# Linear attention with a mixture of experts: the last rounds re-ordered, with one shared expert and eight outputs held back, bulk loads, late stores, and experts shared out by work left

## The chip, the cores and the metric

The kernel runs on one core of one Trainium2 chip. Its time is the device time of one execution in microseconds, and the median of several runs is compared. A profile of one further execution gives the span from the first to the last instruction, and what each engine did in it. TensorE multiplies matrices (PE in the profile; PEld is its loading of weights), VectorE is DVE, ScalarE is ACT, GpSimd is POOL, SyncE is SP. Each engine works through its own instructions in the order written; engines wait for one another by semaphores. All data are 32-bit floats.

## The reference

The input has 4 sequences of 1024 tokens with 256 channels, so 4096 tokens. Each token is normalized, and the result is the sum of the input, an attention block and a feed-forward block, both of the normalized tokens:

```python
xn = _layernorm(x, axis=-1)
x = x + attention(xn, ...) + feed_forward(xn, ...)

# attention: 16 heads of 16 channels
sq, sk = elu(q) + 1, elu(k) + 1
local = causal_linear_attention(q, k, v)        # chunks of 128, running state S and z per head
a_c / n_c                                       # coarse: sum of 4 memory banks, read by sq
out_fine = (outs * softmax(rel)).sum(0)         # the 4 banks one by one, weighed per batch
gprob = sigmoid(relu(coarse @ eg_w1.T + eg_b1) @ eg_w2.T + eg_b2)
memory = gprob * out_fine + (1 - gprob) * coarse
output = (gate * memory + (1 - gate) * local) @ w_o.T

# feed forward: 8 routed experts of 176 hidden channels, the best 2 for each token, and a shared one of 352
cw = two largest of softmax(xn @ gate_weight.T), scaled to sum 1
y = sum over e of cw[e] * (silu(xn @ w_gate[e].T) * (xn @ w_up[e].T)) @ w_down[e].T
y = y + (silu(xn @ sw_gate.T) * (xn @ sw_up.T)) @ sw_down.T
```

## The kernel before

The 4096 tokens are 32 tiles of 128 (`NTT`), and 4 tiles make a block of 512 (`NT`, 8 blocks, `NBLK`). First all blocks are loaded, normalized and transposed; the normalized rows also go to a table `xns` in DRAM. The routing sorts the 8192 pairs of token and expert by expert into 71 groups of 128 slots (`NST`); a group has one expert. A second table in DRAM, `sums`, starts as a copy of the input. Every value tile of a block (`wide`) comes from the pool `big`, tag `tok`, with 8 buffers, one a block.

Then come 34 rounds, one for each tile and two to finish. `attention_round(n)` lists the units of round n: `scores` (TensorE), four `mask`s (DVE), `turned` (transposes for the output of tile n-2 and the gate of tile n-1), `keys_back`, `output(n-2)`, `memory` and `weigh`, `gate_hidden`, `fine`, `local`, `gate_out`, `back` and `update`. Attention has six additions and products on POOL a round: `cg` (in `weigh`), `fm` and two for `diff` (in `fine`), `loc` (in `back`), `state` (in `update`). The score tile `quad` in PSUM is one for all rounds. `output` adds the shared expert's product and the attention's `w_o` product into one PSUM tile. Beside a round stand the key, query and shared-expert projections of the next blocks (`beside`), four rounds for each block, and in rounds 4 to 29 the routed experts (`side`).

A group j of an expert has four steps: `expert_turn` (transposes; it also issues the gather of rows four groups ahead on POOL, `fetch_rows`, L990, and the loads of weights three groups ahead on SP, `fetch_weights`, L1001 to L1009), `expert_hidden` (TensorE, L1036, then ACT and DVE), `expert_out` (TensorE, L1049, then ACT scales it into `y`, three buffers), and `put`. `put` (L1058) is an indirect DMA on POOL that adds the 128 rows of `y` onto `sums`. Two such scatters may hit the same row, so each waits until the one before has landed.

`experts()` lists the units of all groups with weights, `split` cuts the list into 26 parts of equal weight, and `mix` merges lists so that each advances evenly by weight; the merged order is the order in which all engines get their instructions. There is no other scheduler.

The last 8 tiles (from `held_from`, 24) have no `output` in their rounds: their transposed attention `oT` is kept, and the outputs come in the tail, after the last `put`. Tiles before that have their output without the experts in `acc`, held in SBUF. The tail has two kinds of units. `residual(n)` loads a tile's rows of `sums`, and `output(n, True)` adds them and stores the tile from ACT's queue. `experts_part(n)` loads two tiles of `sums` into an expert's weight buffer on SP, and `total(n)` adds them to `acc` on POOL (L980) and at once issues the store on ACT's queue (L981). These totals are mixed evenly over rounds 30 to 33. Every load of `sums` waits for the last `put`.

Of the kernel before, what the change touches and what calls it, by code (L numbers as in the profile page):

```python
# [8 lines left out]
FP = mybir.dt.float32  # L9
# [5 lines left out]
P = 128  # L15
NT = 4
# [6 lines left out]
def linear_attention_moe_kernel(  # L23
# [28 lines left out]
    nc = tc.nc  # L52
    T, H = x.shape
# [3 lines left out]
    NC = H // P  # L57
# [12 lines left out]
    NBLK = T // TB  # L70
    NTT = T // P
# [3 lines left out]
    VW = NH * D1 + CW - D1  # L75
# [19 lines left out]
    st = {}  # L95
# [56 lines left out]
    sums = dram.tile([T + P, H], FP, tag="sums", name="sums")  # L152
# [8 lines left out]
    for e in range(E):  # L161
# [4 lines left out]
        out=before_t, in_=ones, compare_op=ALU.is_gt, fill=0.0,  # L166
# [5 lines left out]
        out=causal, in_=ones, compare_op=ALU.is_ge, fill=0.0,  # L172
# [5 lines left out]
        out=own, in_=ones[:, :HC], compare_op=ALU.is_ge, fill=0.0,  # L178
# [3 lines left out]
        out=own, in_=own, compare_op=ALU.is_ge, fill=0.0,  # L182
# [487 lines left out]
    def at(n):  # L670
        blk, i = divmod(n, NT)
        return blk, i, slice(i * P, (i + 1) * P)
# [180 lines left out]
    def turned(n):  # L853

        srcs = [(s, m) for s, m in (("o", n), ("coarse", n + 1)) if 0 <= m < NTT]
        pt = bank(f"pt2_{n}").rearrange("p (s c t) -> p s c t", s=2, t=P)
        for s, key in enumerate(srcs):
            src = st.pop(key)
            for c in range(NC):
                nc.tensor.transpose(pt[:, s, c, :], src[:, c * P : (c + 1) * P], ident)  # L860
        dst = tmp.tile([P, 2, NC, P], FP, tag="oc", name=f"oc_{n}")
        copied = slice(0, len(srcs))
        if n >= held_from:
            oT = tmp.tile([P, NC, P], FP, tag="oT", name=f"oT_{n}", bufs=NTT - held_from)
            nc.scalar.copy(oT, pt[:, 0])
            copied = slice(1, len(srcs))
        if copied.start < copied.stop:
            nc.scalar.copy(dst[:, copied], pt[:, copied])  # L868
        for s, (what, m) in enumerate(srcs):
            st["oT" if what == "o" else "cT", m] = dst[:, s]  # L870
        if n >= held_from:
            st["oT", n] = oT
# [62 lines left out]
    held_from = NTT - 2 * NT  # L935

    def residual(n):

        res = tmp.tile([P, H], FP, tag="res", name=f"res_{n}", bufs=3)
        nc.sync.dma_start(res, sums[n * P : (n + 1) * P, :])  # L940
        st["res", n] = res

    def output(n, last):

        blk, i, tok = at(n)
        if i == 0:
            st["acc", blk] = io.tile([P, NT, H], FP, tag="xnT", name=f"acc_{blk}")
        acc = st["acc", blk][:, i, :]
        oT = st.pop(("oT", n))
        po = bank(f"po_{n}")  # L950
        for f in range(NF):
            k = min(P, FS - f * P)
            nc.tensor.matmul(  # L953
                po[:, :H], st["h", blk, f][:k, tok], wd[:k, f, :], start=(f == 0), stop=False
            )
        for c in range(NC):
            nc.tensor.matmul(  # L957
                po[:, :H], oT[:, c, :], wo[:, c, :], start=False, stop=(c == NC - 1)
            )
        if last:  # L960
            nc.vector.tensor_add(acc, po[:, :H], st.pop(("res", n)))  # L961
            nc.scalar.dma_start(out[n * P : (n + 1) * P, :], acc)  # L962
        else:
            nc.scalar.copy(acc, po[:, :H])

    def experts_part(n):

        tag, parts = ("wgu", [P, NC, 2, F]) if n % 4 else ("wdn", [P, 2, H])
        flat = "p a b c -> p (a b c)" if n % 4 else "p a b -> p (a b)"
        res = exw.tile(parts, FP, tag=tag, name=f"part_{n}").rearrange(flat)  # L970
        res = res[:, : 2 * H].rearrange("p (n h) -> p n h", h=H)
        nc.sync.dma_start(
            res, sums[n * P : (n + 2) * P, :].rearrange("(n p) h -> p n h", p=P)
        )
        st["part", n] = res

    def total(n):
        blk, i, _ = at(n)
        acc = st["acc", blk][:, i : i + 2, :]
        nc.gpsimd.tensor_add(acc, acc, st.pop(("part", n)))  # L980
        nc.scalar.dma_start(  # L981
            out[n * P : (n + 2) * P, :].rearrange("(n p) h -> p n h", p=P), acc
        )


# [81 lines left out]
    first_round, last_round = 4, 30  # L1067

    def mix(*streams):

        rank = []
        for k, stream in enumerate(streams):
            whole = sum(u[0] for u in stream)
            done = 0
            for u in stream:
                rank.append(((done + u[0] / 2) / whole, k, len(rank), u))
                done += u[0]
        return [u for _, _, _, u in sorted(rank, key=lambda r: r[:3])]

    def run(units):  # L1080
        for _, f, *args in units:
            f(*args)
# [20 lines left out]
    def shared(blk):  # L1103
        units = []
        for f in range(NF):
            units += [
                ((1024, shared_gate, blk, f), None),
                ((1024, shared_up, blk, f), (64, shared_hidden, blk, f)),
            ]
        return units  # L1110
# [10 lines left out]

    def projections(blk):

        pairs = keys(blk) + (queries(blk + 1) if blk + 1 < NBLK else []) + shared(blk)
        units = [u for pair in pairs for u in pair]
        if blk % BPB == 0:
            b = blk // BPB
            at = units.index(pairs[3][1]) + 1
            units[at:at] = [(64, mean_queries, b)]
            at = units.index(pairs[6][0])  # L1130
            units[at:at] = [(64, batch_weights, b)]
        return [u for u in units if u]
# [21 lines left out]
    def experts():  # L1154
        units = [(2000, lambda: None), (256, expert_turn, -2), (256, expert_turn, -1)]
        for j in range(NST + 1):
            if j < NST:
                units += [(704, expert_hidden, j)]
            units += [(64, put, j - 2)] if j > 1 else []
            units += [(512, expert_out, j - 1)] if j > 0 else []  # L1160
            units += [(512, expert_turn, j)] if j < NST else []
        return units + [(64, put, NST - 1)]

    def totals():
        ahead = 5
        pairs = list(range(0, held_from, 2))
        units = [(10, experts_part, n) for n in pairs[:ahead]]
        for k, n in enumerate(pairs):
            if k + ahead < len(pairs):
                units += [(10, experts_part, pairs[k + ahead])]  # L1170
            units += [(64, total, n)]
        return units

    def split(units, parts):

        whole = sum(u[0] for u in units)
        runs = [[] for _ in range(parts)]
        done = 0
        for u in units:
            runs[min(parts - 1, int((done + u[0] / 2) * parts / whole))].append(u)  # L1180
            done += u[0]
        return runs


    ahead = "S0 S1 masks N0 T0 S2 S3 N1 N2 V0 T1 T2 S4 memories V1 S5 N3 N4 V2 T3 T4 S6 gates V3 S7"
# [5 lines left out]
    with tc.tile_pool(name="ps_v", bufs=2, space=bass.MemoryType.PSUM) as ps_v:  # L1191
        for what in ahead.split():
# [3 lines left out]
            blk = int(what[1:])  # L1196
# [31 lines left out]
    rounds = [attention_round(n) for n in range(NTT + 2)]  # L1228
    beside = [[u for pair in shared(1) for u in pair if u]] + [projections(blk) for blk in range(2, NBLK)]
    beside = [units for run_of in beside for units in split(run_of, NT)] + [[]] * (NT + 2)  # L1230
# [12 lines left out]

    side = split(experts(), last_round - first_round)
    for n in range(first_round, last_round):
        run(mix(*[u for u in (rounds[n], beside[n], side[n - first_round]) if u]))

    units = [(10, residual, n) for n in range(held_from, held_from + 3)]  # L1250
    outs = {n: [(1280, output, n, True)] for n in range(held_from, NTT)}
    for n in range(held_from, NTT - 3):
        outs[n] += [(10, residual, n + 3)]
    ready = last_round - 2
    units += [u for n in range(held_from, ready) for u in outs[n]]

    units[2:2] = [(1800, lambda: None)]
    tail = mix([u for n in range(last_round, NTT) for u in rounds[n]], units)

    tail += mix(rounds[NTT], [u for n in range(ready, NTT - 1) for u in outs[n]])  # L1260
    tail += rounds[NTT + 1] + outs[NTT - 1]
    run(mix(tail, totals()))


# [54 lines left out]
```

## Time and profile before

| | |
|---|---|
| median of 3 runs | 736.98 us (736.46 to 739.15) |
| the profiled execution itself | 731.18 us |
| its span, first to last instruction | 729.5 us |
| mean granted clock of TensorE | 0.967 |
| busy: PE, PEld | 653.1, 465.3 us (90%, 64%) |
| busy: DVE, ACT, POOL | 455.9, 266.8, 386.0 us (62%, 37%, 53%) |
| DMA | 81.51 MB, 112 GB/s on the mean |
| scatter `put` L1058 | 71 of 1597 ns on POOL, 113.4 us |
| gather L990 | 71 of 994 ns on POOL, 70.6 us |

How to read it. The page cuts the span into 40 slices of 18.2 us and gives each engine's busy share in tenths; PE has 9 nearly throughout, and 2 in the third slice from the end. A row of groups or of the timeline has the start (timeline only), the busy time, the engine, the line of the kernel, the operation, what it writes and from what, and in brackets the idle time of the engine just before and what ended it. A row of waits has the waiting engine and line, the releaser, the total time, the number of times and the longest. PE's records overlap, since matmuls are pipelined; the spacing of their ends is the truer price. The span of a POOL instruction is rough.

### The profile page before, as it was taken

The page shows a single profiled execution, that of the slowest core. Times are in us where ns is not written, and L with a number is a line of the kernel's source. Part 1 is how long each engine was busy: PE and PEld are TensorE (multiplying, and loading weights), DVE is VectorE, ACT ScalarE, POOL GpSimd, SP SyncE. Part 2 cuts the span into 40 slices and gives each one's busy share as a digit, 9 for nine tenths or more (in the row PEclk, how much of TensorE's full clock was granted, in tenths as well). Part 3 has the DMA queues.
Part 4 walks back from the last instruction along what each step waited for, and adds up shares of the span by engine and source line. Part 5 has one row for each costly group of instructions (what it writes and reads, how often), then busy time and mean ns, then how long its engine had stood idle before and what let it go on. Part 6 is the DMA issues. An engine that isn't in the chain of part 4 may idle for free. (4 is left out here: it accounts for less than half of the span.)

```text
span 729.5 us, 14268 instructions
## 1 busy us (share of the span) xinstructions
PE 653.1 (90%) x5084; PEld 465.3 (64%) x5084; DVE 455.9 (62%) x1193; ACT 266.8 (37%) x614; POOL 386.0 (53%) x436
## 2 busy tenths in 40 slices
PE   3599986879999999999999999999999998997295
PEld 3485465756676776766676767666776665676274
DVE  6444888984656665665666646656666556667262
ACT  3365443423433443334433443344332433333010
POOL 3210034553656675655566666466664656666464
PEclk9799989999999999999999999999999999999598
DMA  9456000013444564454444544454554545552563
GB/s 292 156 198 190 0 1 1 2 52 89 106 116 99 123 127 96 104 119 106 116 116 107 128 109 120 93 129 101 122 126 96 134 112 108 130 127 40 153 200 123
DMA packets 86563, 81.51 MB, mean 112 GB/s; under 512 B 7629, under 2 KB 84093, under 8 KB 86365
## 3 DMA queue, kind: packets, MB, share of 16 engines
q1 hardware_dynamic: 67629, 57.00, 27.3%
q0 software_dynamic: 13632, 18.62, 15.5%
q10 hardware_dynamic: 5232, 4.99, 2.0%
q8 instruction: 40, 0.66, 0.4%
q14 instruction: 30, 0.25, 0.1%
HBM read 62.62 MB, written 22.15 MB: 116 GB/s over the span
## 5 line engine op out<-in xcount | busy, mean ns | idle before, releaser
L1058 POOL DMA_INDIRECT sums<-y,islot x71 | 113.4, 1597 | 70.6 <-DMA sums<-y,islot 15.1
L1042 DVE SCALAR_TENSOR_TENSOR hidden<-hidden,phe 128x176 f32<-128x176 f32 x71 | 23.8, 335 | 122.4 <-ACT hidden L1041 122.4
L1036 PE MATMUL phe<-wgu,turned 128*128 128x352 f32 x276 | 96.9, 474 | 2.5 <-ACT turned L1029 2.1
L698 DVE TENSOR_TENSOR sT<-quad,causal 128x512 f32<-128x512 f32 x128 | 80.4, 681 | 8.3 <-PE quad L691 7.8
L828 POOL TENSOR_TENSOR cg<-coarse,gates 128x256 f32<-128x256 f32 x32 | 24.3, 760 | 109.3 <-DVE h L883 61.1
L990 POOL DMA_INDIRECT xg<-xns,islot x71 | 70.6, 994 | 17.7 <-issue 9.7
L1049 PE MATMUL pye<-wdn,turned 88*128 88x256 f32 x284 | 75.5, 388 | 4.2 <-PE pu L786 3.0
L1036 PEld LDWEIGHTS phe<-wgu,turned 128*128 128x128 f32 x276 | 48.5, 191 | 26.2 <-issue 6.4
L1049 PEld LDWEIGHTS pye<-wdn,turned 88*128 88x128 f32 x284 | 50.1, 189 | 20.1 <-issue 8.5
L1053 ACT ACTIVATE y<-pye,wslot 128x256 f32<-128x256 f32 x71 | 33.6, 473 | 70.6 <-PE pye L1049 70.3
L846 POOL TENSOR_TENSOR fm<-fm 128x512 f32<-128x512 f32 x32 | 41.7, 1304 | 26.2 <-DVE prob L892 13.1
L1041 ACT ACTIVATE hidden<-phe 128x176 f32<-128x176 f32 x71 | 22.6, 318 | 86.7 <-PE phe L1036 79.7
L1029 ACT COPY turned<-pte 128x512 f32<-128x512 f32 (+1 forms) x71 | 41.2, 580 | 35.6 <-PE pte L1027 34.6
L953 PE MATMUL po<-wd,h 128*128 128x256 f32 (+1 forms) x192 | 49.5, 395 | 0.8 <-ACT oc L868 0.7
L905 PE MATMUL pg<-xnT,wg 128*128 128x512 f32 (+1 forms) x96 | 48.2, 627 | 0.0
L919 PE MATMUL psu<-xnT,wu 128*128 128x512 f32 (+1 forms) x96 | 46.1, 603 | 0.5 <-DVE loc L751 0.5
L835 DVE TENSOR_TENSOR fm<-quad,rw 128x512 f32<-128x512 f32 x64 | 42.2, 680 | 0.0
L953 PEld LDWEIGHTS po<-wd,h 128*128 128x128 f32 (+1 forms) x192 | 35.8, 196 | 7.7 <-ACT oc L868 1.2
L362 PE MATMUL pv<-wvg,xnT 128*128 128x264 f32 x128 | 33.1, 420 | 8.2 <-ACT xnT L347 8.2
L560 POOL TENSOR_TENSOR held<-ones,two 128x213 f32<-128x213 f32 (+1 forms) x22 | 16.0, 737 | 44.5 <-DVE ones L540 44.5
L806 PE MATMUL quad<-mem,sqT 32*128 32x170 f32 x512 | 27.6, 328 | 9.1 <-DVE sT L698 9.1
L894 DVE SCALAR_TENSOR_TENSOR o<-diff,prob,loc 128x256 f32<-128x256 f32 x32 | 33.1, 1035 | 3.4
(210 smaller groups left out, 1374.5 us busy)
## 6 DMA issues: line engine op xcount, KB each, us to landing
wgu<-in_w_gate_dram SPq DMA_DIRECT2D x71, 176.0 KB
wgu<-in_w_up_dram SPq DMA_DIRECT2D x71, 176.0 KB
wdn<-in_w_down_dram SPq DMA_DIRECT2D x71, 176.0 KB
x<-in_x_dram SPq DMA_DIRECT2D x8, 512.0 KB
xns<-x SPq DMA_DIRECT2D x8, 512.0 KB
sums<-in_x_dram SPq DMA_DIRECT2D x8, 512.0 KB
part<-sums SPq DMA_DIRECT2D x12, 256.0 KB
out_dram<-acc ACTq DMA_DIRECT2D x12, 256.0 KB
```

The lines of the kernel that those rows point to most:

```text
L698: nc.vector.tensor_mul(sT, quad[:, g, :].rearrange("p (c t) -> p c t", t=P), causal[:, None, :].to_broadcast([P, NC * 2, P]),)
L835: nc.vector.tensor_mul(fm[:, c].rearrange("p g m (r k) -> p g (m r) k", k=HD), quad[:, :, c * KM + KX + KN : (c + 1) * KM].rearrange("p g ...
L846: nc.gpsimd.tensor_add(fm[:, :, 0:2, :], fm[:, :, 0:2, :], fm[:, :, 2:4, :])
L905: nc.tensor.matmul(pg[:n, :], wg[:, k, f * P : f * P + n], xnT[:, k, :], start=(k == 0), stop=(k == NC - 1),)
L919: nc.tensor.matmul(pu[:n, :], wu[:, k, f * P : f * P + n], xnT[:, k, :], start=(k == 0), stop=(k == NC - 1),)
L953: nc.tensor.matmul(po[:, :H], st["h", blk, f][:k, tok], wd[:k, f, :], start=(f == 0), stop=False)
L990: nc.gpsimd.indirect_dma_start(out=xg, out_offset=None, in_=xns, in_offset=bass.IndirectOffsetOnAxis(ap=islot[:, j : j + 1], axis=0),)
L1029: nc.scalar.copy(dst[:, lo:hi], pt[:, lo:hi])
L1036: nc.tensor.matmul(ph[:, : 2 * F], xgT[:, k, :], wgu[:, k].rearrange("p g f -> p (g f)"), start=(k == 0), stop=(k == NC - 1),)
L1049: nc.tensor.matmul(py[:, :H], hT[:FH, f, :], wdn[:, f, :], start=(f == 0), stop=(f == 1))
L1053: nc.scalar.activation(y, py[:, :H], AF.Copy, scale=wslot[:, j : j + 1])
L1058: nc.gpsimd.indirect_dma_start(out=sums, out_offset=bass.IndirectOffsetOnAxis(ap=islot[:, j : j + 1], axis=0), in_=st.pop(("y", j)), in_of ...
```

## The change

- The shared expert of the last block (`shared(7)`) is no longer among the projections beside rounds 24 to 27; it is mixed with round 30.
- The experts are cut by work left: each round from 4 to 29 gets as many weight units of experts as it lacks to a common level, at most 1.5 times the mean.
- All loads of `sums` are issued together after round 29: two residual loads of four tiles each, then twelve loads of two tiles.
- Residuals, the kept `oT` and six of the twelve parts are placed in buffers of the early value tiles (`big`, tag `tok`); the other six parts stay in expert weight buffers (`in_weights`).
- No total stands in round 30. They are mixed evenly over what follows round 30, and their stores are on SP's queue, each behind the next total. The eight outputs follow in rounds 31, 32 and 33 (three, three, one, and the last by itself), and each of their stores is on ACT's queue, one output later.

```diff
@@ -861,7 +861,9 @@
         dst = tmp.tile([P, 2, NC, P], FP, tag="oc", name=f"oc_{n}")
         copied = slice(0, len(srcs))
         if n >= held_from:
-            oT = tmp.tile([P, NC, P], FP, tag="oT", name=f"oT_{n}", bufs=NTT - held_from)
+            if n % NT == 0:
+                st["oTs"] = big.tile([P, NT, VW], FP, tag="tok", name=f"oT_{n}")
+            oT = st["oTs"][:, n % NT, : NC * P].rearrange("p (c t) -> p c t", t=P)
             nc.scalar.copy(oT, pt[:, 0])
             copied = slice(1, len(srcs))
         if copied.start < copied.stop:
@@ -936,9 +938,12 @@
 
     def residual(n):
 
-        res = tmp.tile([P, H], FP, tag="res", name=f"res_{n}", bufs=3)
-        nc.sync.dma_start(res, sums[n * P : (n + 1) * P, :])
-        st["res", n] = res
+        res = big.tile([P, NT, VW], FP, tag="tok", name=f"res_{n}")[:, :, :H]
+        nc.sync.dma_start(
+            res, sums[n * P : (n + NT) * P, :].rearrange("(n p) h -> p n h", p=P)
+        )
+        for i in range(NT):
+            st["res", n + i] = res[:, i]
 
     def output(n, last):
 
@@ -959,27 +964,38 @@
             )
         if last:
             nc.vector.tensor_add(acc, po[:, :H], st.pop(("res", n)))
-            nc.scalar.dma_start(out[n * P : (n + 1) * P, :], acc)
         else:
             nc.scalar.copy(acc, po[:, :H])
 
     def experts_part(n):
 
+        if n < 3 * NT:
+            if n % NT == 0:
+                st["parts"] = big.tile([P, NT, VW], FP, tag="tok", name=f"part_{n}")
+            res = st["parts"][:, n % NT : n % NT + 2, :H]
+        else:
+            res = in_weights(n)
+        nc.sync.dma_start(
+            res, sums[n * P : (n + 2) * P, :].rearrange("(n p) h -> p n h", p=P)
+        )
+        st["part", n] = res
+
+    def in_weights(n):
         tag, parts = ("wgu", [P, NC, 2, F]) if n % 4 else ("wdn", [P, 2, H])
         flat = "p a b c -> p (a b c)" if n % 4 else "p a b -> p (a b)"
         res = exw.tile(parts, FP, tag=tag, name=f"part_{n}").rearrange(flat)
-        res = res[:, : 2 * H].rearrange("p (n h) -> p n h", h=H)
-        nc.sync.dma_start(
-            res, sums[n * P : (n + 2) * P, :].rearrange("(n p) h -> p n h", p=P)
-        )
-        st["part", n] = res
+        return res[:, : 2 * H].rearrange("p (n h) -> p n h", h=H)
 
     def total(n):
         blk, i, _ = at(n)
         acc = st["acc", blk][:, i : i + 2, :]
         nc.gpsimd.tensor_add(acc, acc, st.pop(("part", n)))
-        nc.scalar.dma_start(
-            out[n * P : (n + 2) * P, :].rearrange("(n p) h -> p n h", p=P), acc
+
+    def store(n, tiles, queue):
+        blk, i, _ = at(n)
+        queue.dma_start(
+            out[n * P : (n + tiles) * P, :].rearrange("(n p) h -> p n h", p=P),
+            st["acc", blk][:, i : i + tiles, :],
         )
 
 
@@ -1121,7 +1137,8 @@
 
     def projections(blk):
 
-        pairs = keys(blk) + (queries(blk + 1) if blk + 1 < NBLK else []) + shared(blk)
+        pairs = keys(blk) + (queries(blk + 1) if blk + 1 < NBLK else [])
+        pairs += shared(blk) if blk + 1 < NBLK else []
         units = [u for pair in pairs for u in pair]
         if blk % BPB == 0:
             b = blk // BPB
@@ -1161,23 +1178,18 @@
             units += [(512, expert_turn, j)] if j < NST else []
         return units + [(64, put, NST - 1)]
 
-    def totals():
-        ahead = 5
-        pairs = list(range(0, held_from, 2))
-        units = [(10, experts_part, n) for n in pairs[:ahead]]
-        for k, n in enumerate(pairs):
-            if k + ahead < len(pairs):
-                units += [(10, experts_part, pairs[k + ahead])]
-            units += [(64, total, n)]
-        return units
-
     def split(units, parts):
 
+        if isinstance(parts, int):
+            parts = [1] * parts
+        ends = [sum(parts[: i + 1]) / sum(parts) for i in range(len(parts))]
         whole = sum(u[0] for u in units)
-        runs = [[] for _ in range(parts)]
-        done = 0
+        runs = [[] for _ in parts]
+        done, at = 0, 0
         for u in units:
-            runs[min(parts - 1, int((done + u[0] / 2) * parts / whole))].append(u)
+            while at < len(parts) - 1 and done + u[0] / 2 > ends[at] * whole:
+                at += 1
+            runs[at].append(u)
             done += u[0]
         return runs
 
@@ -1243,23 +1255,39 @@
 
 
 
-    side = split(experts(), last_round - first_round)
+
+    def weight(units):
+        return sum(u[0] for u in units)
+
+    work = experts()
+    share = [weight(rounds[n]) + weight(beside[n]) for n in range(first_round, last_round)]
+    level = max(share)
+    cap = 1.5 * weight(work) / len(share)
+    while sum(min(cap, max(0, level - s)) for s in share) < weight(work):
+        level += 10
+    side = split(work, [min(cap, max(0, level - s)) for s in share])
     for n in range(first_round, last_round):
         run(mix(*[u for u in (rounds[n], beside[n], side[n - first_round]) if u]))
 
-    units = [(10, residual, n) for n in range(held_from, held_from + 3)]
+
     outs = {n: [(1280, output, n, True)] for n in range(held_from, NTT)}
-    for n in range(held_from, NTT - 3):
-        outs[n] += [(10, residual, n + 3)]
-    ready = last_round - 2
-    units += [u for n in range(held_from, ready) for u in outs[n]]
-
-    units[2:2] = [(1800, lambda: None)]
-    tail = mix([u for n in range(last_round, NTT) for u in rounds[n]], units)
-
-    tail += mix(rounds[NTT], [u for n in range(ready, NTT - 1) for u in outs[n]])
-    tail += rounds[NTT + 1] + outs[NTT - 1]
-    run(mix(tail, totals()))
+    for n in range(held_from + 1, NTT):
+        outs[n] += [(10, store, n - 1, 1, nc.scalar)]
+    loads = [(10, residual, n) for n in range(held_from, NTT, NT)]
+    loads += [(10, experts_part, n) for n in range(0, held_from, 2)]
+    sums_of = []
+    for n in range(0, held_from, 2):
+        sums_of += [(64, total, n)]
+        sums_of += [(10, store, n - 2, 2, nc.sync)] if n else []
+    sums_of += [(10, store, held_from - 2, 2, nc.sync)]
+    run(loads)
+
+    run(mix(rounds[last_round], [u for pair in shared(NBLK - 1) for u in pair if u]))
+    tail = mix(rounds[last_round + 1], [u for n in range(held_from, NTT - 5) for u in outs[n]])
+    tail += mix(rounds[NTT], [u for n in range(NTT - 5, NTT - 2) for u in outs[n]])
+    tail += mix(rounds[NTT + 1], outs[NTT - 2]) + outs[NTT - 1]
+    run(mix(tail, sums_of))
+    store(NTT - 1, 1, nc.scalar)
 
 
 # ---- launch: one core; weights laid out with the contracted channel first ----
```

More of the change, by code (lines that the diff above doesn't have):

```diff
@@ L966, in experts_part @@
     def experts_part(n):
-        tag, parts = ("wgu", [P, NC, 2, F]) if n % 4 else ("wdn", [P, 2, H])
-        flat = "p a b c -> p (a b c)" if n % 4 else "p a b -> p (a b)"
-        res = exw.tile(parts, FP, tag=tag, name=f"part_{n}").rearrange(flat)
-        res = res[:, : 2 * H].rearrange("p (n h) -> p n h", h=H)
+        if n < 3 * NT:
[4 more added lines that the diff above has]
+            res = in_weights(n)
         nc.sync.dma_start(
@@ L975, in experts_part @@
         st["part", n] = res
+    def in_weights(n):
+        tag, parts = ("wgu", [P, NC, 2, F]) if n % 4 else ("wdn", [P, 2, H])
+        flat = "p a b c -> p (a b c)" if n % 4 else "p a b -> p (a b)"
+        res = exw.tile(parts, FP, tag=tag, name=f"part_{n}").rearrange(flat)
+        return res[:, : 2 * H].rearrange("p (n h) -> p n h", h=H)
     def total(n):
```

## The prediction

> **What bounds the kernel now.** Four views, in this order. First the busy time by stretch, 620 us to the end (PE, PEld, DVE, ACT and POOL busy, then granted clock, DMA share, GB/s):
>
> ```profile
> 620.00:640.00 20.00, 19.61 (x157) 13.26 (x158) 14.17 (x33) 7.11 (x17) 14.12 (x14) 1.00 0.52 125
> 660.00:680.00 20.00, 13.40 (x148) 10.22 (x147) 14.22 (x34) 4.40 (x12) 13.09 (x13) 0.94 0.25 28
> 680.00:690.00 10.00, 0.95 (x5) 0.95 (x5) 0.00 (x0) 1.14 (x3) 4.08 (x5) 0.50 0.67 178
> 690.00:700.00 10.00, 8.93 (x65) 7.05 (x64) 4.87 (x13) 1.18 (x3) 4.54 (x6) 0.77 0.68 215
> ```
>
> Up to 640 TensorE sets the pace (98% busy); then comes a hole. Who waits in it, from the waits of 640 to 729.5 (total us, times, longest):
>
> ```profile
> ACT oT L865 <- POOL acc L980: 22.5, 2, 15.8
> PE ph L879 <- ACT oc L868: 14.4, 2, 12.0
> ```
>
> The timeline gives its order:
>
> ```profile
> 679.09 1.56 POOL L1058 DMA_INDIRECT sums<-y,islot  x1 [2.13 <-issue]
> 682.81 0.84 SPq L940 DMA_DIRECT2D res<-sums  x2
> 683.75 4.46 SPq L972 DMA_DIRECT2D part<-sums  x7
> 686.57 2.48 POOL L980 TENSOR_TENSOR acc<-acc,part 128x512 f32<-128x512 f32 x2 [5.92 <-DMA part<-sums]
> 687.86 0.46 ACTq L981 DMA_DIRECT2D out_dram<-acc  x1
> 688.36 0.37 ACT L865 COPY oT<-pt 128x256 f32<-128x256 f32 x1 [15.83 <-POOL acc L980]
> 689.05 1.12 PE L879 MATMUL ph<-w,oc 128*128 128x64 f32 x4 [11.96 <-ACT oc L868]
> ```
>
> The last scatter (`put`, L1058) lands at 682.8; only then may SP load, POOL add, and ACT issue the store of `total(0)`. That store stands in ACT's queue ahead of the copy of round 30, so ACT, then PE, stop. The chain of waits gives TensorE's price of full work:
>
> ```profile
> 698.21 1.30 PE po L953 x6
> 699.51 0.86 PE po L957 x4
> ```
>
> Ten matmuls of 256 columns in 2.16 us: 0.216 each, 0.84 ns a column. Last, POOL, which the change loads more:
>
> ```profile
> 600.31 1.61 POOL L1058 DMA_INDIRECT sums<-y,islot  x1 [0.16 <-issue]
> 602.22 0.99 POOL L990 DMA_INDIRECT xg<-xns,islot  x1 [0.30 <-issue]
> 603.23 1.27 POOL L846 TENSOR_TENSOR fm<-fm 128x512 f32<-128x512 f32 x1
> ...
> 606.75 0.76 POOL L797 TENSOR_TENSOR state<-state,state 128x272 f32<-128x272 f32 x1
> 607.67 1.59 POOL L1058 DMA_INDIRECT sums<-y,islot  x1 [0.15 <-issue]
> ...
> 674.60 1.57 POOL L1058 DMA_INDIRECT sums<-y,islot  x1 [0.15 <-issue]
> 675.62 1.34 POOL L797 TENSOR_TENSOR state<-state,state 128x272 f32<-128x272 f32 x1
> 679.09 1.56 POOL L1058 DMA_INDIRECT sums<-y,islot  x1 [2.13 <-issue]
> ```
>
> A scatter, a gather and a round's five additions (0.7 to 0.8 us each but for `fm`) cost 7.36 us. Scatters with one small addition between stand 4.5 apart (674.60 to 679.09), since each waits for the one before to land: 3.7 to 5.3 us after its start, median 4.0, in the scatter's own view, then some 0.5 more.
>
> [...]
>
> **The change, part by part.** Prices first. Twenty-three rounds (5 to 27) take 455.5 us by their first masks (190.1 to 645.6), 19.8 each. An attention round without output is 5.6 by the pieces of the chain (scores 1.1, transposes 0.6, memory 0.8, gate 0.5, local 1.1, back 1.1, update 0.4); an output 2.16; projections and shared expert 40 matmuls of 512 columns a block, 10 x 0.43 = 4.3 a round. What is left of 19.8 for 2.78 experts (71 over 26 rounds, weighed) is 2.8 us each; by columns 2.5.
>
> *Experts by work left.* The units' weights put 2.35 to 2.5 experts into rounds 4 to 23 (2.78 before), 3.55 and 3.7 into 24 and 25, 4.18 into 26 to 29. In POOL's order, 57 scatters stand before round 25's `cg` addition now, 51 afterwards; before round 30's, 71 in both. TensorE sets the pace till then, so round 25's `cg` (599.4) comes earlier by 6 experts x 2.8 = 16.8, plus two pairs of shared-expert matmul groups not yet done, 3.5: at 579.1.
>
> From there 20 scatters are due in five rounds, and POOL takes over. Their 19 gaps, by the new queue order: three gaps with gather and four additions, 6.6 each; one with gather and three, 5.9; fifteen with little between, 4.5 to 4.75. Sum 96. TensorE for the same: 5 x 5.6, one output, 20 x 2.8, projections 3.5, so 90. With landings 0.2 slower under 1.5 times the weight traffic and a little waiting for DVE I take 102. Bounds: 96, and 116 at 6.1 a gap, the point of the slower rival below. The last scatter starts at 580 + 102 = 682 and lands near 686. **The last landing hardly moves** (682.8 before): the 20 us gained are given back to the scatter chain.
>
> *Shared expert of block 7 to round 30, stores behind.* What changes is what TensorE has done by then. Three `y` buffers let it run some 10 us ahead of the scatters; round 30 holds 5.6 + 24 x 0.43 = 15.9 us that need no `sums`, only the state addition just ahead of the last scatter, for `back`. Scatter 67's landing (682 - 13.7 + 4 = 672) frees the last `y`; from 671 on, `y` being ScalarE's and not TensorE's wait at first, this work covers the landing and ends near 687. Without this cover TensorE would stand 12 us again.
>
> *The eight held outputs.* All now follow: 8 x 2.16 = 17.3, round 31 5.1, leftovers of 32 and 33 1.5: 24 us after 687. DVE has output 24's addition ahead of round 31's masks, so masks wait for `res_24`: SP issues (0.45) and 512 KB land by about 689.5. Output 24 and round 31's scores, 3.3 us, cover it. End of TensorE 687 + 24 = 711, plus 1.5 of joints; from the last output's matmul to the end 3.4 now (726.1 to 729.5), the same after: **span 716**.
>
> *Loads and stores.* 14 loads (2 of 512 KB, 12 of 256) are issued together: no SP instruction is behind them but the stores. The DMA view of the first 30 us has 360 to 388 GB/s while loads of the same rows run: 4.2 MB take 12 us and 4.2 MB of stores as much: done by 711 even one after the other, behind TensorE. ACT's single stores follow one output later, 0.4 us each, no wait. POOL: twelve totals of 1.26 = 15 us beside round 31's 5 us, in 24; four totals stand ahead of round 31's `cg`: parts land from 691, so `cg` is near 696, `diff` near 702, `o` near 704, due at 709. Cover 5 us; beyond it every us counts in full.
>
> *Buffers.* `oT`, residuals and parts take seven of the eight value buffers in turn; their last readers are rounds of blocks 0 to 6, finished by round 27. Nothing.
>
> Sum: 729.5 - 716 = 13.5 us. The profiled execution took 731.2 itself, the median of the runs is 736.98, 0.8% more; the difference is carried over: **723.5 us**.
>
> **Rivals.** *Slower: the scatter chain stretches.* For no gain the last scatter must start at 695.5, that is 19 gaps of 6.1 us on average where I have 5.4. Speaking for it: steady rounds had gaps of 8.2 with the additions between. Against: those waited for TensorE (4.6 and 2.9 us before `cg`), and 642 to 679 ran at 5.26. At 6.5 the span is 737.5, time 745: the end follows the last landing one for one. *Half of it*: landings at 4.5 throughout (median 4.0, slowest 5.3), 14 gaps x 0.5 = 7 us: last scatter 689, span 723, time 730.5. *No POOL limit*: if TensorE's 90 us rule, span 706, time 713; against it the 4.5 us floor. *The tail is bound by totals*: parts late by 8 us make `o` of round 31 late by 3, time 727.
>
> **How the numbers follow.** Forecast (time 717 to 728) 0.62; half 0.12; no limit 0.09; totals 0.06; slower 0.11. Low 714 takes in most of the no-limit case, high 734 the half case and its neighbours. 0.5% is 3.7 us, about what a measurement of this kernel tells from no change. Faster 0.85: forecast, totals, no limit and two thirds of half; same 0.06: the rest of half and the edge of slower; slower 0.09.
>
> **What would show it.** The hole at 680 gone and the clock at 1.00 there; ACT never behind L980. The last scatter between 677 and 690, gaps of 4.5 to 6.6 over the last 20. PE busy from 671 to 711. Round 25's `cg` near 579. Wrong if `cg` of 25 isn't earlier by 15 or more, if gaps exceed 6, or if DVE waits for `res` beyond 692.

## The result, and the profile after

| | before | changed |
|---|---|---|
| median | 736.72 us, 4 runs (735.52 to 739.15) | 725.6 us, 4 runs (720.73 to 728.15) |
| the profiled execution, its span | 731.18, 729.5 us | 720.73, 718.8 us |
| last `put` starts | 679.09 us | 682.76 us |
| first scores of round 31 | 700.3 us | 687.1 us |
| TensorE ends | 726.1 us | 713.9 us |

The ratio is 0.9855, with an interval of 0.9816 to 0.9893: faster by 1.5%. The forecast was 723.5 us. In the profiled executions 10.7 us were gained where the sum had said 13.5.

The busy time by stretch (PE, PEld, DVE, ACT and POOL busy, then granted clock, DMA share, GB/s), changed kernel:

```profile
580.00:600.00 20.00, 18.10 (x162) 13.73 (x162) 11.61 (x33) 9.27 (x22) 14.20 (x14) 1.00 0.65 152
600.00:620.00 20.00, 15.06 (x94) 10.60 (x93) 7.94 (x20) 4.59 (x11) 14.65 (x14) 0.76 0.65 144
...
680.00:690.00 10.00, 10.00 (x98) 6.74 (x97) 8.06 (x20) 1.76 (x4) 7.16 (x8) 1.00 0.44 89
690.00:700.00 10.00, 7.53 (x78) 6.26 (x77) 5.85 (x15) 0.65 (x2) 5.55 (x6) 1.00 1.09 377
```

The hole is gone: 680 to 690 has TensorE busy throughout at a granted clock of 1.00, where before it was busy for 0.95 us at 0.50. But 600 to 620 now has a dent: 15.06 us busy, clock 0.76 (before: 17.26 and 0.91). The loads of `sums` stand in one block from 687 on, at 377 GB/s over 690 to 700.

Timeline of the changed kernel around the last scatter, the same instructions as shown of before:

```profile
682.76 1.56 POOL L1074 DMA_INDIRECT sums<-y,islot  x1 [2.11 <-DVE h L887]
686.57 0.94 SPq L942 DMA_DIRECT2D res<-sums  x2
687.55 7.67 SPq L978 DMA_DIRECT2D part<-sums  x12
690.63 0.42 DVE L966 TENSOR_TENSOR acc<-po,res 128x256 f32<-128x256 f32 x1 [1.44 <-PE po L962]
690.97 2.47 DVE L698 TENSOR_TENSOR sT<-quad,causal 128x512 f32<-128x512 f32 x4
692.46 4.59 POOL L992 TENSOR_TENSOR acc<-acc,part 128x512 f32<-128x512 f32 x4 [3.02 <-DMA part<-sums]
693.50 0.86 PE L806 MATMUL quad<-mem,sqT 32*128 32x170 f32 x16 [2.47 <-DVE sT L698]
695.61 18.38 SPq L996 DMA_DIRECT2D out_dram<-acc  x12
```

The last landing is 3.8 us later than before (the first loads start at 686.57 for 682.81), and nothing but POOL's first total waits for it. ACT no longer stands behind a total (L992). What is left of the old hole is 2.47 us of TensorE, in which the masks of round 31 run late: DVE's addition of output 24 stands ahead of them and waits for its `po`.

The chain of waits ends in the outputs, at the price that the prediction took:

```profile
709.19 1.30 PE po L958 x6
710.49 0.86 PE po L962 x4
```

POOL's timeline where scatters set the pace, as shown of before:

```profile
579.48 0.72 POOL L828 TENSOR_TENSOR cg<-coarse,gates 128x256 f32<-128x256 f32 x1 [0.57 <-DVE h L885]
581.31 1.61 POOL L1074 DMA_INDIRECT sums<-y,islot  x1 [1.11 <-ACT hidden L1057]
583.22 0.99 POOL L1006 DMA_INDIRECT xg<-xns,islot  x1 [0.30 <-issue]
584.24 1.27 POOL L846 TENSOR_TENSOR fm<-fm 128x512 f32<-128x512 f32 x1
...
587.96 1.60 POOL L1074 DMA_INDIRECT sums<-y,islot  x1 [0.16 <-issue]
...
678.29 1.57 POOL L1074 DMA_INDIRECT sums<-y,islot  x1 [3.42 <-DMA sums<-y,islot]
682.76 1.56 POOL L1074 DMA_INDIRECT sums<-y,islot  x1 [2.11 <-DVE h L887]
```

Round 25's `cg` is at 579.48 (599.42 before). From there 20 scatters have 19 gaps of 4.4 to 7.3 us, 5.34 on the mean; the one with a gather and four additions is 6.65.

What was not foreseen is in the waits of 560 to 680 (total us, times, longest); the kernel before has neither a wait of TensorE for gathered rows nor one of ACT for a result buffer there:

```profile
ACT y L1069 <- DMA sums<-y,islot: 10.2, 4, 2.8
PE pte L1043 <- DMA xg<-xns,islot: 6.3, 4, 3.7
```

So with the scatters close together TensorE waits for the rows of experts, since POOL gets to the gathers late.

### The profile page after: what moved, and what is told of

Same layout as the page of the kernel before. It is cut to its first block, busy times and chain, and to the rows that moved or that the text cites. A ratio compares the mean times of both kernels' runs of the same rounds, so it can differ in the third digit from the quotient of the medians.

```text
span 718.8 us, 14242 instructions
## 1 busy us (share of the span) xinstructions
PE 656.1 (91%) x5084; PEld 468.4 (65%) x5084; DVE 455.8 (63%) x1193; ACT 266.9 (37%) x614; POOL 385.6 (54%) x436
## 4 chain that ended last, share of the span: by engine, by line
PE 71%; DMA 9%; DVE 8%; POOL 4%; ACT 4%; issue 3%; SPq 0%; ACTq 0%; POOLq 0%; DVEq 0%
PE phe L1052 11%; PE pye L1065 7%; PE psu L921 6%; PE po L958 6%; PE pg L907 5%; DMA sums<-y,islot 4%; PE quad L691 4%; PE pn L717 4%; PE po L962 4%; PE quad L806 3%; PE pk L600 3%; PE pq L600 3%; PE pv L362 2%; PE pte L1039 2%; PE pte L1043 2%
## 5 line engine op out<-in xcount | busy, mean ns | idle before, releaser
L1052 PE MATMUL phe<-wgu,turned 128*128 128x352 f32 x276 | 99.5, 484 | 2.5 <-ACT turned L1045 1.2
L1058 DVE SCALAR_TENSOR_TENSOR hidden<-hidden,phe 128x176 f32<-128x176 f32 x71 | 23.8, 335 | 117.8 <-ACT hidden L1057 113.2
L1065 PE MATMUL pye<-wdn,turned 88*128 88x256 f32 x284 | 77.3, 395 | 1.8 <-issue 1.4
L846 POOL TENSOR_TENSOR fm<-fm 128x512 f32<-128x512 f32 x32 | 44.0, 1374 | 26.7 <-DVE prob L894 16.6
L958 PE MATMUL po<-wd,h 128*128 128x256 f32 (+1 forms) x192 | 47.4, 383 | 0.1
L896 DVE SCALAR_TENSOR_TENSOR o<-diff,prob,loc 128x256 f32<-128x256 f32 x32 | 37.4, 1167 | 3.4
```

Source lines behind the costliest of these rows:

```text
L846: nc.gpsimd.tensor_add(fm[:, :, 0:2, :], fm[:, :, 0:2, :], fm[:, :, 2:4, :])
L958: nc.tensor.matmul(po[:, :H], st["h", blk, f][:k, tok], wd[:k, f, :], start=(f == 0), stop=False)
L1052: nc.tensor.matmul(ph[:, : 2 * F], xgT[:, k, :], wgu[:, k].rearrange("p g f -> p (g f)"), start=(k == 0), stop=(k == NC - 1),)
L1065: nc.tensor.matmul(py[:, :H], hT[:FH, f, :], wdn[:, f, :], start=(f == 0), stop=(f == 1))
```

## The experiments

Each kernel was timed against the kernel before on the same chip, whose median there was 731.5, 732.4 or 732.6 us, lower than on the chip of the first comparison; so ratios are compared, not times. Two accounts are to be told apart. *Mine*: the tail's order removes the hole, the shared expert held back covers the landing, and the cut by work left is about neutral, because what it gains early it gives back to the chain of scatters. *The rival*: the cut by work left costs time, and the tail alone brings the gain. Spans and single instructions are those of one profiled execution of each kernel.

| kernel | ratio to before, interval | median, us | last `put` starts | first scores of round 31 |
|---|---|---|---|---|
| before | 1 | | 679.1 | 700.3 |
| changed | 0.9855 (0.9816 to 0.9893) | 725.6 | 682.8 | 687.1 |
| before, with the cut by work left alone | 1.0116 (1.0079 to 1.0153) | 738.1 | 684.5 | 705.7 |
| changed, with the even cut of before | 0.9728 (0.9697 to 0.9759) | 711.4 | 670.7 | 675.7 |
| the tail's new order alone | 0.9845 (0.9822 to 0.9869) | 719.4 | 676.9 | 682.2 |
| changed, totals from round 30, stores at once on ACT | 1.015 (1.0128 to 1.0172) | 742.2 | 679.9 | 700.6 |
| the same, stores on SP | 0.9883 (0.9863 to 0.9903) | 724.3 | 683.7 | 689.9 |
| changed, gathers earlier | 0.9826 (0.9802 to 0.9849) | 719.0 | 681.0 | 685.1 |
| changed, two tables of sums | 0.995 (0.9931 to 0.9969) | 728.4 | 679.5 | 689.6 |
| changed, one table, start of two | 1.0088 (1.0059 to 1.0117) | 737.8 | 694.2 | 700.0 |
| even cut, output 24 added later | 0.9655 (0.9632 to 0.9679) | 707.1 | 670.9 | 678.6 |
| the same, gathers earlier | 0.9652 (0.9628 to 0.9676) | 707.1 | 670.5 | 680.3 |

**The cut by work left, alone.** The kernel before with only the new `split` and its levels:

```diff
-    side = split(experts(), last_round - first_round)
+    side = split(work, [min(cap, max(0, level - s)) for s in share])
```

> Kernel before with the new cut of the experts alone; the tail, loads and stores are those of before. Theory (what TensorE gains early is given back to the scatter chain): round 25's cg addition comes some 11 us earlier than in before, the last scatter still starts at 679 to 685, the hole behind it stays at 12 us; time 736 to 740, ratio 1.000 to 1.005. Rival (the cut by work left is itself a gain, because rounds 28 and 29 are filled): 730 to 733.

It is slower by 1.2%, where 0.5% at most was expected. The last scatter starts 5.4 us later (684.5 for 679.1), the span is 5.7 us longer (735.2), and the hole follows it, a little wider: TensorE's longest wait in it is 14.8 us for 12.0.

**The changed kernel with the even cut.**

```diff
-    side = split(work, [min(cap, max(0, level - s)) for s in share])
+    side = split(work, len(share))
```

> The changed kernel with the experts cut evenly again; everything else stays. Theory: without a dense end of 20 scatters in five rounds the last scatter starts near 671 instead of 683, TensorE reaches output 24 at 686 instead of 690.6, time 719 to 723, a few us below the changed kernel's 725.6. Rival (levelled rounds are part of the gain): 729 to 733.

Undoing that one line makes the changed kernel 1.3% faster still (0.9728 over 0.9855 is 0.987), in agreement with the run before it, and more than I had expected. The last scatter starts 12.1 us earlier, where it was expected (671), and output 24 is added at 679.23 for 690.63. By the first masks of the rounds, the levelled cut is 22.0 us ahead at round 24 (548.0 for 570.1), and then takes 125.9 us for rounds 24 to 29 where the even cut takes 92.2. Of the 33.7 us more, 22.0 are the work moved there; the others are lost. The chain of waits that ends last shows where: in the changed kernel it runs through seven landings of scatters between 571 and 672 us, 29.6 us in all, and with the even cut through none. (A chain of waits is read back from the last instruction, at each step to what it waited for.) The last of the seven frees a result buffer, and round 30 stands behind it:

```profile
667.84 3.75 DMA sums<-y,islot
671.63 0.04 issue
671.67 0.47 ACT y L1069
672.15 0.40 ACT skO L678
```

Round 31 itself runs worse with the even cut, and this is the timeline of TensorE in it:

```profile
682.11 1.52 PE L806 MATMUL quad<-mem,sqT 32*128 32x170 f32 x16 [2.47 <-DVE sT L698]
683.55 2.93 PE L958 MATMUL po<-wd,h 128*128 128x256 f32 x6
686.27 1.92 PE L962 MATMUL po<-wo,oT 128*128 128x256 f32 x4
```

After the 2.47 us wait for masks the products take about twice the time (2.93 for 1.56 us, 1.92 for 1.03; the granted clock is 0.66 over 680 to 690), and part of what the earlier landing gave is lost: the span is 8.5 us shorter than the changed kernel's, not 12.

**The tail's new order alone.** The even cut, and the last block's shared expert back beside rounds 24 to 27; round 30 stands alone:

```diff
-        pairs += shared(blk) if blk + 1 < NBLK else []
+        pairs += shared(blk)
...
-    run(mix(rounds[last_round], [u for pair in shared(NBLK - 1) for u in pair if u]))
+    run(rounds[last_round])
```

> The tail alone: loads issued together, totals from round 31 on with stores behind, outputs later; block 7's shared expert is back beside rounds 24 to 27 and the experts are cut evenly. Prediction's step (without the shared expert as cover TensorE stands some 12 us again): 734 to 738. Second theory (what stopped TensorE was ACT's store in the queue, and round 30 with scores and output 24 covers most of the landing by itself; a wait of 3 to 4 us for the residual is left, and from output 24's addition the same 28 us follow as in the changed kernel): 720 to 725.

The tail's order by itself brings 1.55%, as much as the whole change. So the prediction's cover of 12 us isn't needed in that size. The chain of waits of this kernel from the last scatter (676.86) on shows why:

```profile
676.80 1.87 PE pn L717 x32
...
678.75 0.59 ACT nT L724
...
679.39 1.11 PE pb L733 x4
680.50 0.91 PE pb L739 x4
681.41 0.91 PE pu L786 x4
682.31 1.75 PE quad L691 x32
684.06 1.50 PE po L958 x6
685.55 0.88 PE po L962 x4
686.43 0.02 issue
686.46 0.42 DVE acc L966
```

No DMA stands in it. The rest of round 30, the scores of round 31 and output 24's products take the 9.6 us between the scatter's start and the first use of `sums`, and all of that can run without `sums`. Round 30 has 2.3 us of idle TensorE, and round 31 the same 2.5 us for masks. Holding the shared expert back is worth 1.2% on top (0.9728 for 0.9845), and not by 12 us of cover for the landing. TensorE has less to do before the last scatter, which starts 6.2 us earlier, and the work comes back in round 30, where it fills waits of the round itself. Here that round takes 11.0 us from its first scores to those of round 31 (671.2 to 682.2). With the shared expert in it, and the even cut, it takes 15.0 (660.7 to 675.7), of which 9.0 are the shared expert's matmuls: some 5 us less for the rest. Of these, 2.3 are the idle time; the others are slower products behind it, up to 683: the granted clock is 0.84 over 670 to 680 and 0.82 over 680 to 690, and with the shared expert held back 1.00 over 660 to 680. The same products, first here, then with the shared expert held back:

```profile
676.73 1.91 PE L717 MATMUL pn<-sT,x 128*32 128x128 f32 x32
...
669.68 1.08 PE L717 MATMUL pn<-sT,x 128*32 128x128 f32 x32
```

**Totals mixed from round 30 on, each store at once on ACT's queue**, as before; all else as changed:

```diff
-        sums_of += [(64, total, n)]
-        sums_of += [(10, store, n - 2, 2, nc.sync)] if n else []
-    sums_of += [(10, store, held_from - 2, 2, nc.sync)]
+        sums_of += [(64, total, n), (10, store, n, 2, nc.scalar)]
...
-    run(mix(rounds[last_round], [u for pair in shared(NBLK - 1) for u in pair if u]))
-    tail = mix(rounds[last_round + 1], ...)
+    tail = mix(rounds[last_round], [u for pair in shared(NBLK - 1) for u in pair if u])
+    tail += mix(rounds[last_round + 1], ...)
```

> The changed kernel with the totals mixed in from round 30 on and each store issued at once on ACT's queue, as before the change. Theory: ACT stands at the first store until the first part has landed and is added (about 694), TensorE follows it some 2 us later, round 30's shared expert is late: time 736 to 742. Rival (the place of the stores is of no weight, the loads and the shared expert made the gain): 724 to 728.

The hole is back, and the 16 us of shared-expert work in round 30 don't fill it. The waits of 640 to the end, then the stretch 680 to 690:

```profile
ACT oT L867 <- POOL acc L992: 19.2, 1, 19.2
PE ph L881 <- ACT oc L870: 13.8, 2, 12.2
...
680.00:690.00 10.00, 0.00 (x0) 0.00 (x0) 0.00 (x0) 0.00 (x0) 1.87 (x2) 0.64 0.62 188
```

ACT waits 19.2 us at a store, and TensorE does nothing for a whole 10 us: behind the store stand the very copies and activations that the work of round 30 needs.

**The same totals from round 30, but stored from SP, behind the next total.**

```diff
-        sums_of += [(64, total, n), (10, store, n, 2, nc.scalar)]
+        sums_of += [(64, total, n)]
+        sums_of += [(10, store, n - 2, 2, nc.sync)] if n else []
+    sums_of += [(10, store, held_from - 2, 2, nc.sync)]
```

> The changed kernel with the totals mixed in from round 30 on, but their stores on SP's queue behind the next total, so that ACT never waits for them. Theory (the order on ACT made the hole): most of the loss of the run with stores on ACT goes, 727 to 731 where that run had 742 and the changed kernel 725.6; what is left is POOL standing at the first total ahead of round 30's attention additions. Rival (POOL's order makes the hole by itself): 738 to 742.

Moving the stores alone, to SP's queue and one total later, gives back 2.6% (0.9883 for 1.015). POOL now waits at its first total, with the additions of attention behind it, and the ratio is within 0.3% of the changed kernel's; the two intervals overlap:

```profile
POOL acc L992 <- DMA part<-sums: 8.2, 1, 8.2
```

So the place of the stores made the hole, and POOL's order costs little. How much of it is the queue and how much the one total later was not separated.

**Gathers earlier.** The dent at 600 could be the price of late gathers. Five buffers for the gathered rows, and each gather issued six groups ahead for four:

```diff
...
-        xg = exp.tile([P, H], FP, tag="xg", name=f"xg_{j}", bufs=3)
+        xg = exp.tile([P, H], FP, tag="xg", name=f"xg_{j}", bufs=5)
...
-        fetch_rows(j + 4)
+        fetch_rows(j + 6)
...
```

> The changed kernel, with each group's gather of rows issued two groups earlier (six ahead, five buffers). Theory A (in rounds 26 to 29 TensorE stands for gathers that stand behind scatters on POOL; four waits of 6.3 us in all, and the clock falls after each to 0.76 to 0.9, some 8 us more): the waits for the gather go, the clock stays at 1.00, time 8 to 13 us below the changed kernel, ratio to before 0.968 to 0.975. Theory B (the chain of scatters itself is the limit, through the three result buffers; the gather only passes it on): at most 3 us, ratio 0.982 to 0.986.

The waits for gathers go, and come back one buffer further on; waits of 560 to 680:

```profile
ACT y L1069 <- DMA sums<-y,islot: 40.7, 13, 4.8
```

ScalarE now waits 40.7 us for a result buffer, which a scatter has to free, where the changed kernel had 10.2. The first theory had the clock fall after each of the four waits. In the changed kernel it fell after two: behind 3.69 us it is 0.50 over 612 to 624, behind 2.17 us 0.50 over 656 to 658; behind waits of 0.21 and 0.25 us it is 1.00 (603.6 to 608 and 660 to 664). With the gathers earlier it is 0.91 over 620 to 640 and over 660 to 680, and 1.00 in the rest of 560 to 680. The gaps of the scatters are nearly the same, 4.4 to 6.8 us and 5.16 on the mean for 5.34, and so is the span (718.5 for 718.8). The ratio differs by 0.3%, and the two intervals overlap.

**Two tables of sums.** If each scatter's wait for the one before is the limit, two chains must be faster than one. Groups of odd number add into a second table that nothing reads, so the output lacks their share; the table is filled at the start like the first, 4 MB more. The control has the second table and its filling, but every scatter goes to the first.

```diff
...
+        nc.sync.dma_start(other_sums[rows, :], x[rows, :])
...
-            out=sums,
+            out=other_sums if j % 2 else sums,
...
```

> The changed kernel, with the scatters of odd groups going to a second table that nothing reads (their part is left out of the output), so that a scatter waits for the one before the last. Theory A and B both: gaps of the dense scatters fall from 4.5 to 7 us to about 4, the last scatter starts near 668 to 674 instead of 683. Theory B: ratio to before 0.968 to 0.976. Theory A: gathers no longer stand behind a waiting scatter either, the same gain; it would be refuted if gaps fell and the time did not. Rival C (the loss of the new cut is contention of weights and scatters in the DMA engines): gaps stay above 5, ratio 0.983 to 0.988.

> The changed kernel with the second table of the run before, made by the same extra copies at the start (4 MB), but with every scatter going to the first table, so that the output is whole again. It tells what the copies cost by themselves. If the chain of scatters sets rounds 24 to 29 of the changed kernel, these rounds take some 126 us here as in the changed kernel (118 with two tables), and the time is 733 to 738, that is 6 to 10 us over the two tables. If the copies have no lasting cost, or two tables gained for another reason, the time is 724 to 729 with rounds 24 to 29 as short as with two tables.

Alone, the two tables don't answer the question: the filling puts the kernel back by 10 us and more from the first experts on. By first masks, round 24 starts at 558.5 us with two tables, 561.6 in the control and 548.0 in the changed kernel. Set against the control they do: the ratio of the two is 0.995 over 1.0088, 0.986. Rounds 24 to 29 take 117.8 us with two tables, 125.0 in the control, 125.9 in the changed kernel. Of the 12.1 us between the two spans (721.3 and 733.4) 7.2 are in these six rounds; the starts differ by 3.2, and the tail by the rest. The waits of POOL for a scatter and most of TensorE's for a gather are gone. Control, waits of 560 to 680:

```profile
POOL sums L1075 <- DMA sums<-y,islot: 16.2, 9, 3.0
...
PE pte L1044 <- DMA xg<-xns,islot: 11.7, 7, 3.1
```

In the same stretch two tables have one wait of TensorE for a gather, 3.2 us, and 0.3 us of POOL for a scatter. Start to start, no two scatters of the control are closer than 4.35 us; with two tables the closest are 1.9 to 3.2. The chain of waits that ends last agrees: after round 24 it runs through nine landings of scatters in the control, and through none with two tables. So the chain of scatters does hold up the levelled rounds, by some 7 us. The even cut's last scatter is 12.1 us earlier than the changed kernel's. What makes the other 5 wasn't separated; over these rounds the granted clock is 0.93 in the changed kernel, 1.00 with the even cut, and 0.97 in both kernels of this pair.

**Output 24 added later.** The 2.47 us for masks come from DVE's order. On top of the even cut, output 24's addition goes behind the masks of round 31:

```diff
...
+    def first_added():
+        nc.vector.tensor_add(
+            st["acc", held_from // NT][:, 0, :], st.pop("po")[:, :H], st.pop(("res", held_from))
+        )
...
+    outs[held_from] += [(400, lambda: None), (10, first_added)]
```

> The even cut with the rest of the change, and output 24's addition on DVE moved behind round 31's four masks. Theory: the wait of 2.5 us of TensorE for the masks goes, and with it the fall of the clock that cost some 3 us in the next products: 2.5 to 6 us below the even cut alone, ratio to before 0.965 to 0.970. Rival (the residual's landing or the chain of round 31 sets the pace there anyway): within 1 us, ratio 0.972 to 0.974.

```profile
680.09 2.47 DVE L698 TENSOR_TENSOR sT<-quad,causal 128x512 f32<-128x512 f32 x4
682.48 0.40 DVE L973 TENSOR_TENSOR acc<-po,res 128x256 f32<-128x256 f32 x1
682.61 0.86 PE L806 MATMUL quad<-mem,sqT 32*128 32x170 f32 x16
683.40 1.56 PE L958 MATMUL po<-wd,h 128*128 128x256 f32 x6
```

In this timeline of DVE and TensorE the masks run first, the products that follow them start right behind the last mask without a wait in the record, and they keep their full speed (a granted clock of 1.00 over 680 to 690). The time is 707.1 us, 3.45% below before, and the span is 4.0 us shorter than with the even cut. From the first scores of round 31 to the end it is 6.9 us shorter (27.7 for 34.6): about 2.4 by the wait, 3.1 by the products behind it, which have their full speed again, and 1.2 after the last product. Round 31 starts 2.9 us later in this profiled execution (678.6 for 675.7), though the last scatter doesn't and the edit touches nothing before it. The kernel beats both others.

**The same, with gathers earlier.** The edit is the one shown.

> The even cut with output 24's addition moved behind the masks (707.1 us, ratio 0.9655), and in addition the gathers six groups ahead in five buffers instead of four ahead in three. With the even cut TensorE idles only 7 us in rounds 24 to 29, and not for gathers alone. If gathers late on POOL are still a cost there: 1 to 3 us less, 704 to 706. If each wait only moves on to the result buffers, as with the levelled cut: within 1.5 us of 707.

Nothing: 707.13 for 707.08 us. The gathers aren't a limit with the even cut either.

## Why the prediction was right, and where it was not

The forecast of 723.5 us is within 0.3% of the median. By its steps:

- **Experts by work left: the sizes were right, the judgement was not.** Round 25's `cg` at 579.1 (measured 579.48), gaps of 5.4 on the mean (5.34), the landing that frees the last `y` at 672 (671.6), the last scatter at 682 (682.76). The 0.2 us for slower landings was an allowance of the author's; the seven landings in the chain of waits take 4.23 us on the mean (29.6 over 7) where the median before was 4.0, and whether the weights' traffic does that was not separated. The step that failed is "The last landing hardly moves: the 20 us gained are given back to the scatter chain", as a verdict on this part. It set the landing of the whole change against the kernel before, and so counted as neutral a part that costs 1.2 to 1.3%, alone or with the rest. The shared expert held back takes some 10 us (24 x 0.43) of work out of rounds 24 to 27, and with it and the even cut the last scatter is at 670.7. The levelled cut spends that: it moves experts out of rounds where the scatters have gaps of up to 14.5 us with the even cut, in which the chain has room to spare, and into rounds where they stand 4.4 to 7.3 apart; the gaps of the last 20 scatters average 5.3 us in the changed kernel, 6.2 with the even cut and 6.6 before. That the gathers go late then, and TensorE waits and slows (0.76 over 600 to 620), was seen by no step.
- **The shared expert as cover.** "Without this cover TensorE would stand 12 us again" failed: without it TensorE idles 2.3 us in round 30, and some 5 in all with the slower products behind them. Those 12 us were the wait for a copy behind a store in ACT's queue, and the prediction gave the cure to the wrong edit; with the stores back on ACT the hole stands in spite of the cover. The start of round 31, priced at 687, was 687.06: the sum of TensorE's work held, the reason given for the edit's worth did not.
- **Stores on SP, one total later.** Right, and the largest part: 2.6% between the two kernels that differ in it alone.
- **Masks behind output 24.** The order was seen and called covered: `res_24` by 689.5, and it didn't hold DVE up; what did was TensorE's own end of output 24 at 690.6, so 2.47 us stood where 1.5 us of joints had been allowed. TensorE ended at 713.9, not 712.5: this and the next step are the whole miss of the span, 718.8 for 716.
- **The end after the last product.** 3.4 us was carried over from before; it is 4.9 in the changed kernel and with the even cut, 3.7 with output 24's addition moved. What makes the 1.5 us wasn't tried.
- **Loads, stores, buffers.** Right: 14 loads are issued in 8.6 us (686.57 to 695.2) and run at 377 GB/s; SP's twelve stores wait behind them only until 695.6. No wait for a value buffer shows. That the stores on SP's queue would come behind its loads was the author's assumption; in the trace SP's first store starts at 695.61 us, behind its last load.

Of the rivals, *totals* came nearest: the first total waits 3.0 us for its part, and `cg` of round 31 is at 699.0 for 696, but TensorE's outputs filled the time. The slower one needed gaps of 6.1 where 5.34 were measured. *No POOL limit* was summed wrong: 90 us for 102 is 12 us less, a span of 704 and not 706; nothing rests on it.

## What to carry to other kernels

In this kernel a store in the queue of an engine that also computes held up everything behind it (ACT stood for 15.8 us before, for 19.2 us with totals from round 30 and stores on ACT). If a store waits for a chain that ends late, put it on a queue where nothing stands behind, before looking for work to cover the wait. When work feeds a serial chain (here scatters that wait for one another), balance the chain first and the compute second: here work moved late to fill an engine came out as a later end of the chain. And judge each part with the other parts in place: a last landing that hardly moves for the whole change can hide one part that spends what another gained.

## What was not expected of the hardware

- An idle stretch of TensorE of the same length had two outcomes. In the changed kernel the products after 2.47 us for masks ran at full speed (0.86 us for 16 small ones at 693.50, 1.56 us for six of `po`; the granted clock is 1.00 over 690 to 700); with the even cut after 2.47 us they took 1.52 and 2.93 (0.66 over 680 to 690). Slow products also came behind a shorter wait: with the tail's order alone, after 1.58 us for masks, the 16 small ones still took 0.86 us at 675.35, but from 676.73 to 683 products were slower (1.91 us for 1.08 in L717). What decides between the outcomes was not found.
- After 3.69 us of waiting for a gather the changed kernel's expert products took 2.55 us for 1.35, then 2.66 at 620.69, and 1.35 again only at 626.10:

```profile
603.92 1.35 PE L1052 MATMUL phe<-wgu,turned 128*128 128x352 f32 x4
...
611.35 0.69 PE L1043 MATMUL pte<-ident,xg 128*128 128x128 f32 x2 [3.69 <-DMA xg<-xns,islot]
...
612.68 2.55 PE L1052 MATMUL phe<-wgu,turned 128*128 128x352 f32 x4
```

The granted clock is 0.50 throughout 612 to 624, though TensorE is busy for 95% of that stretch (11.36 of 12 us). At a clock of 1.00 the same work would take about half of that: by this estimate some 5.7 us were lost behind a wait of 3.7.
- The closest two scatters that add to one table are 4.46 us apart, start to start, in the kernel before, 4.38 in the changed kernel and 4.35 in the control of the two tables; the 4.38 (663.46 to 667.84) has one small addition of POOL between. Alternating between two tables they come as close as 1.9.
